# A pre-norm decoder layer on one core: residual rows loaded behind the second weights, cross results stored and norms read back later, weight making begun later, more ternary comparisons in the first batch

## The chip, the cores and the metric

The kernel runs on 1 core of a Trainium2 chip. The core has a matrix engine (PE, TensorE), a vector engine (DVE, VectorE), a scalar engine (ACT, ScalarE), a general engine (POOL, GpSimd) and a synchronising engine (SP, SyncE). Each takes its instructions in the order in which the program gives them to it; a wait holds everything behind it on the same engine. SP and POOL here issue the DMA transfers, which 16 DMA engines carry out. The metric is device time of one execution in microseconds (us), lower is better.

## What is computed

The reference is a decoder layer with a norm ahead of each of its three parts, for x and a context ctx of 4 batches x 512 rows x 512 features, all in 32-bit floats (cut to what matters):

```
x = x + self_attention(layernorm(x))       # 16 heads of 128, Wq Wk Wv Wo with biases
x = x + gamma * cross(layernorm(x), ctx)   # keys and values are both ctx
x = x + ffn(layernorm(x))                  # ternary weights

# self_attention: q, k, v = x @ W + b, shaped (heads, 128, T); the attention runs over
#   the features: att = softmax(q @ k / sqrt(128)) is 128x128 per head; y = att @ v; y @ Wo + bo
# cross: 8 heads over blocks of 64 rows: softmax((q.T @ k) / sqrt(64)), 512x512 per head, times v
# ffn: silu(x @ w1q.T) * (x @ w3q.T), then @ w2q.T, hidden size 1365
# ternary: q = clip(round(w / s), -1, 1) * s with s = mean(abs(w)), for w1, w3 and w2
```

## The kernel before

The work is done in this order, with times of the profile of before.

*First phase, 0 to about 289 us.* Norms of x, Gram matrices, keys and scores of the four batches. Beside it, on "ticks" (a generator is advanced by so many steps at so many places of the main work; the class `Side` counts them), `kept_weights` (L296 to L337) makes the weights Wo and Wv ready: each row piece is loaded by SP (L205), split into a high part h (ACT, L277), a low part l and a third part d (DVE), and the three parts are stored by SP to scratch (`kept`). It is advanced KEPT_STEPS = 64 steps over 80 ticks. `scale_steps` sums the absolute values of the ternary matrices (ACT, L636). PE turns and multiplies the Gram matrices; `gt` (L475) needs the copy of G by ACT (L438).

*The batch loop, about 289 to 820 us* (b = 0 to 3, in each four groups of heads j = 0 to 3). For every (b, j), `values_out` makes the products `pu` with the parts oh, ol, od of Wo, `values_of` makes `pm` with vh, vl, vd of Wv, and `output` (L567 to L573) adds `po` to the four accumulators `acc`. The twelve loads of 256 KB for each product are issued on SP by `weights`, into a pool of 20 buffers. The accumulators start as the rows of x (`accumulators`: four loads on SP) with the bias bo, broadcast by a fifth load of 256 KB and added by DVE (`biased`, L1034). eT, the turned scores, comes back by SP (`turned_kept`). u, ul, ud and m are made by DVE, uh by ACT.

A product has 6 ticks, so a batch has 48. On these ticks three things run beside the main work: the making of ternary weights, the norms of the batch before, and its cross-attention.

- `ternary_steps` (L653 to L670): a load on POOL (L605), two comparisons on DVE (L660, L661), then a step further a store on POOL (L669). In all 70 steps over the 180 ticks from the first product on.
- `row_norms` (L686 to L702): statistics of the accumulators on DVE, a store of the norms on POOL (`norm_a`), and two reads back on POOL (`norms`).
- `cross(b)` (L704 to L845): all its transfers go through POOL (L713): `fetch` loads xd (rows of x) and kd (rows of the context) for a head, `split` makes qs, kh and kl of them with the norms (ACT L733 and L737, DVE L734 and L738), `softmax_rows` does the scores `xs` (PE L750, L751), their maximum (DVE), the exponentials p (ACT L761) and the division, `transpose_rows` turns p (PE, then a copy to pt by ACT L131 or DVE L133), `turn_values` turns the rows `keys` into `vals` (one buffer), `weigh_values` multiplies them (`xo`, L794) and adds the residual rows `xc` (DVE L802), and `store` writes the result to x_c. Every 4 scores make one such result; c counts the results, `phase` the scores in it. The loads `keys` and `xc` share one kind of buffer ("late").

The last cross-attention and the feed-forward part (L1183, L1192, L1221) run from about 820 to 1141 us.

The parts of the order around the change that matter: SP issues in the order acc, bo, weights vh.. of the first product, eT, weights oh.. of the second one; POOL issues in the order in which the generators are advanced.

Of the kernel before, what the change touches and what calls it, by code (L numbers as in the profile page):

```python
# [19 lines left out]
P = 128  # L20
B, T, D = 4, 512, 512
NC = T // P
KC = D // P
# [18 lines left out]
def decoder_layer_kernel(  # L42
# [161 lines left out]
    def load(dst, src):  # L204
        nc.sync.dma_start(dst, src)  # L205
        return dst
# [89 lines left out]
    def kept_weights(pool):  # L296

        def items():
            for j in range(HG):
                for k in range(KC):  # L300
                    yield "o", j, k, None
                for k in CHUNKS:
                    yield "v", j, k, None

        sources = {}

        def bring(n, j, k):
            if n == "o":
                t = pool.tile([P, GW], F32, tag="raw_v", bufs=4, name=f"o_raw_{j}_{k}")
                load(t, by_group(wo[j * T : (j + 1) * T, :], k))  # L310
                return t
            if k == KC - 1:
                sources[j] = raw_of("v", j, pool, load, 4)
            return sources[j][1](k)

        coming = []
        for item in itertools.chain(items(), [None, None]):
            if item is not None:
                coming.append((item[:3], bring(*item[:3])))
                if len(coming) < 3:  # L320
                    continue
            (n, j, k), t = coming.pop(0)
            gate = gates[0]
            if n == "v":
                fold(k, t, sources[j][0], gate)
            tri = Tri(
                *(pool.tile([P, GW], F32R, tag="made", bufs=4, name=f"{n}{p}_{j}_{k}") for p in "hl"),
                t.bitcast(F32R),
            )
            halves_of_weight(tri.h, tri.l, t, gate)  # L330
            third_of_weight(tri)
            yield
            for p, part in zip("hld", (tri.h, tri.l, tri.d)):
                load(kept[n, j, p][ts(k, P), :], part.bitcast(F32))
            yield

    KEPT_STEPS = 2 * 2 * HG * KC  # L337

    def weights(n, b, j, wp):

        def part(p, k):
            t = wp.tile([P, GW], F32R, tag="w", name=f"{n}{p}_{b}_{j}_{k}")
            load(t.bitcast(F32), kept[n, j, p][ts(k, P), :])
            return t

        halves = [(part("h", k), part("l", k)) for k in range(KC)]
        return [Tri(*halves[k], part("d", k)) for k in range(KC)]
# [327 lines left out]
    def each(steps, stp):  # L675
        for name in MATRICES:
            yield from steps(stp, name)
# [8 lines left out]
    def row_norms(b, accs):  # L686


        mv = small.tile([P, NG, 2], F32, tag="mvc", bufs=2, name=f"mv_c_{b}")
        for g in range(NG):  # L690
            yield
            moments(mv[:, g, :], accs[g], f"c_{b}_{g}")
        rstd = rstd_of(mv, f"c_{b}")
        mean, var = (mv[:, :, i : i + 1].rearrange("p c s -> p (c s)") for i in range(2))
        nc.vector.tensor_scalar(mean, mean, -1.0, None, ALU.mult)
        nc.vector.tensor_copy(var, rstd)
        nc.gpsimd.dma_start(norm_a[b].rearrange("(p g) s -> p g s", g=NG), mv)
        norms[b] = small.tile([P, 2 * NC, 2], F32, tag="norms", bufs=2, name=f"norms_{b}")
        for half in (slice(0, XD), slice(XD, P)):
            nc.gpsimd.dma_start(norms[b][half], norm_a[b].rearrange("(n p) s -> p n s", p=XD))  # L700
        for _ in range(NG + 3):
            yield  # L702

    def cross(b, cx, cin, cpp, cpt):  # L704
# [11 lines left out]
        def late(name, src):  # L716
            return load(cx.tile([P, T], F32, tag="late", name=f"{name}_{b}"), src)
# [70 lines left out]
        def weigh_values(c, xc):  # L788
            pt = [pts.pop(2 * c + j) for j in range(2)]
            po = bank(f"xo_{b}_{c}")  # L790
            for l in range(NC):
                for j in range(2):
                    half = slice(j * XD, (j + 1) * XD)
                    nc.tensor.matmul(  # L794
                        po[half, :],
                        lhsT=vals[c][:, l, half],
                        rhs=pt[j][:, l, :],
                        start=(l == 0),
                        stop=(l == NC - 1),
                    )  # L800
            y = vals.pop(c).rearrange("p l d -> p (l d)")
            nc.vector.scalar_tensor_tensor(y, po, gam, xc, ALU.mult, ALU.add)  # L802
            return lambda: load(x_c[b][ts(c, P), :], y)
# [14 lines left out]
        for i in range(len(order) + 3):  # L818
            c, phase = divmod(i, 4)
            if phase == 3 and c < NC:  # L820
                rows[c] = late(f"keys_{c}", kv[b][ts(c, P), :])
            if i < len(order):
                ps[order[i]] = softmax_rows(*order[i])
            if i < len(order):
                yield
            if phase == 2 and c > 0:
                store = weigh_values(c - 1, rows.pop(c - 1))
                yield
            if 2 <= i < len(order) + 2:
                n, h = order[i - 2]  # L830
                transpose_rows(n, h, ps.pop((n, h)))
            if i % 2 == 0 and i // 2 + 1 < heads:
                split(i // 2 + 1)
            if i % 2 == 0 and i // 2 + 2 < heads:
                fetch(i // 2 + 2)
            if phase == 2 and c > 0:
                store()
            if i < len(order) + 2:
                yield
            if phase == 0 and c > 0:  # L840
                turn_values(c - 1)
            if phase == 1 and c > 0:
                rows[c - 1] = late(f"xc_{c - 1}", x_a[b][ts(c - 1, P), :])
            if i < len(order) + 2:
                yield  # L845
# [177 lines left out]
    def accumulators(b):  # L1023
        accs = []
        for g in range(NG):
            acc = accp.tile([P, D], F32, tag="acc", name=f"acc_{b}_{g}")
            load(acc, by_group(x[b], g))
            accs.append(acc)
        return accs
# [5 lines left out]

    PRODUCT = 6
    TICKS = 2 * HG * PRODUCT
    quant, aside, side = Side(), Side(), Side()
    waiting, accs = None, None

# [11 lines left out]
    def turning():  # L1052
        count = itertools.count(1)

        def tick():
            at = next(count)
            if at in (4, 6):
                turn(len(STEPS) - 4 + at // 2)

        return tick  # L1060

    for b in range(B):
        for j in range(HG):
            if b == 0 and j == 0:
                wo_tiles = weights("o", b, j, wp)
                accs = accumulators(0)
                load(bo_bc, bo.to_broadcast([P, D]))
            else:
                if j == HG - 1 and b + 1 < B:
                    next_accs = accumulators(b + 1)  # L1070
                wo_tiles = weights("o", b, j, wp)
            u3 = values_out(b, j, x3, wo_tiles, tick if b + j > 0 else turning())
            if b == 0 and j == 0:
                quant = Side(each(ternary_steps, stp), 2 * PIECES, B * TICKS - 2 * PRODUCT)
            if waiting:
                output(*waiting)
            if j == 0 and b > 0:
                aside.rest()
                crossing = itertools.chain(row_norms(b - 1, accs), cross(b - 1, *cpool))
                aside = Side(itertools.islice(crossing, AHEAD), AHEAD, (3 if b == 1 else 2) * PRODUCT)  # L1080
                accs = next_accs
            if j == 1 and b > 1:
                begin_cross(TICKS)
            if j == HG - 2:
                xs = rows_kept(b + 1, xnp, "xn")
            if j == HG - 1 and b + 1 < B:
                x3 = parts_of(b + 1, xs)
            elif j == HG - 1:
                for t in xs:
                    settle(t)  # L1090
                ffn_0 = prepare_ffn(0, xs)
                for _ in range(NC):
                    next(ffn_0)
            wv_tiles = weights("v", b, j, wp)
            eT = turned_kept(b, j)
            ms = values_of(b, j, wv_tiles, u3, tick)
            if j == 0:
                biased(accs)
            if j == 1 and b == 1:
                begin_cross(TICKS - PRODUCT)  # L1100
            waiting = [b, j, eT, ms, accs]
# [177 lines left out]
```

## Time and profile before

| | us |
|---|---|
| three runs | 1147.08, 1142.03, 1145.89 |
| median of them | 1145.89 |
| profiled execution, its own time | 1143.08 |
| its span in the profile | 1141.3 |
| PE busy | 1124.5 |
| DVE, ACT, POOL busy | 808.1, 562.4, 204.1 |

The profiled execution lies 2.81 us below the median of the runs, and its span 1.8 us below its own time. An engine's busy time leaves out waits; the weight loads of PE (PEld) run beside its products. In a list of waits a row names the engine and line that waited, what ended the wait last, and then total us, number and longest. A timeline row gives start, duration, engine, line, operation, output and inputs, the number of instructions joined in the row, and in brackets the idle time before the first of them with what ended it. SPq and the rows of POOL with DMA_DIRECT2D are issues of transfers; a transfer lands some us later.

The 16 DMA engines are 90% and more busy in many of the 40 slices of the first 830 us, 70 to 80% in most others (q1, the queue of SP, carries 187.48 MB, q0, that of POOL, 63.50 MB over the whole span), and mostly 10 to 20% busy after that.

### The profile page before, as it was taken

What the parts mean: (1) busy time and instruction counts of PE and PEld (TensorE: products, weight loads), DVE (VectorE), ACT (ScalarE), POOL (GpSimd) and SP (SyncE); (2) the same over time, 40 slices, a digit from 0 to 9 for tenths busy, and PEclk for the clock granted to TensorE, in tenths of its full rate; (3) what the DMA queues carried; (4) which work ended last, traced back from release to release, by engine and by line L of the source; (5) the groups of instructions that cost most, each with busy time, mean ns of one, the idle gap of its engine ahead of it and who ended that gap; (6) DMA issues with size and microseconds to landing.
All of it is one profiled execution on the core that took longest, in us unless ns stands there. A gap on an engine that the chain in (4) does not pass through costs nothing.

```text
span 1141.3 us, 16617 instructions
## 1 busy us (share of the span) xinstructions
PE 1124.5 (99%) x5406; PEld 874.1 (77%) x5406; DVE 808.1 (71%) x1616; ACT 562.4 (49%) x1200; POOL 204.1 (18%) x377
## 2 busy tenths in 40 slices
PE   9999999999999999999999999999999999999998
PEld 6778888888777777777767777577677877778886
DVE  7678676865556786898778788696887669537252
ACT  5375545553322334665646565465566557434020
POOL 2011001010111132232223213221222212000000
PEclk9999999999999999999999999999999999999999
DMA  9257879794999899978779977896941422121200
GB/s 308 80 177 242 277 251 327 241 326 149 386 351 384 302 316 332 332 231 299 240 221 333 319 235 255 252 332 224 328 152 65 148 65 65 47 74 37 93 1 37
DMA packets 145844, 252.04 MB, mean 221 GB/s; under 512 B 17032, under 2 KB 48008, under 8 KB 145758
## 3 DMA queue, kind: packets, MB, share of 16 engines
q1 hardware_dynamic: 124830, 187.48, 48.6%
q0 software_dynamic: 20928, 63.50, 17.4%
q8 instruction: 43, 0.70, 0.2%
q14 instruction: 43, 0.35, 0.1%
HBM read 196.37 MB, written 54.54 MB: 220 GB/s over the span
## 4 chain that ended last, share of the span: by engine, by line
PE 80%; DMA 7%; DVE 5%; issue 5%; ACT 2%; POOL 1%; SPq 0%; POOLq 0%; DVEq 0%; ACTq 0%
PE h L1183 13%; PE y L1221 7%; PE sc L529 5%; PE xo L794 4%; PE xp L128 4%; PE po L570 3%; PE xs L750 2%; PE xs L751 2%; DMA kd<-in_kv_dram 2%; PE pm_2d L368 1%; PE pu_0h L357 1%; PE pm_3h L356 1%; PE pu_3h L356 1%; PE pu_0d L368 1%; PE py_3h L356 1%
## 5 line engine op out<-in xcount | busy, mean ns | idle before, releaser
L1183 PE MATMUL h<-fxh,t 128*128 128x512 f32 (+1 forms) x352 | 139.8, 397 | 0.0
L1183 PE MATMUL h<-fxl,t 128*128 128x512 f32 (+1 forms) x352 | 137.5, 390 | 0.0
L761 ACT ACTIVATE p<-xs,xnmax 128x512 f32<-128x512 f32 x128 | 86.9, 686 | 94.9 <-PE xp L128 55.2
L755 DVE TENSOR_REDUCE xnmax<-xs 128x1 f32<-128x512 f32 x128 | 84.7, 681 | 2.8 <-PE xs L751 2.8
L1183 PEld LDWEIGHTS h<-fxh,t 128*128 128x128 f32 (+1 forms) x352 | 65.0, 185 | 16.4 <-issue 1.9
L1183 PEld LDWEIGHTS h<-fxl,t 128*128 128x128 f32 (+1 forms) x352 | 65.0, 185 | 14.6 <-DVE fxl L141 0.4
L1221 PE MATMUL y<-t,gh 128*128 128x512 f32 (+1 forms) x176 | 69.3, 394 | 0.0
L1221 PE MATMUL y<-t,gl 128*128 128x512 f32 (+1 forms) x176 | 68.8, 391 | 0.0
L128 PEld LDWEIGHTS xp<-ident,p 128*128 128x128 f32 x512 | 59.0, 140 | 11.2 <-issue 2.4
L131 ACT COPY pt<-xp 128x512 f32<-128x512 f32 x96 | 54.3, 590 | 26.5 <-PE xp L128 26.5
L128 PE MATMUL xp<-ident,p 128*128 128x128 f32 x512 | 66.4, 273 | 0.1
L713 POOL DMA_DIRECT2D xd<-x_a x64 | 33.7, 531 | 169.5 <-DVE qs L734 112.8
L1192 ACT ACTIVATE th<-h,scales_w 128x512 f32<-128x512 f32 (+1 forms) x44 | 30.4, 691 | 65.7 <-PE h L1183 65.5
L529 PE MATMUL sc<-y,q_raw 128*128 128x128 f32 x512 | 59.3, 275 | 0.0
L529 PEld LDWEIGHTS sc<-y,q_raw 128*128 128x128 f32 x512 | 58.4, 192 | 0.2
L570 PE MATMUL po<-m,eT 128*128 128x512 f32 x128 | 58.1, 595 | 0.4 <-DVE u L378 0.4
L794 PE MATMUL xo<-pt,vals 128*64 128x512 f32 x256 | 58.5, 598 | 0.0
L197 ACT ACTIVATE uh<-u 128x512 fp32r<-128x512 f32 x64 | 40.2, 632 | 28.2 <-DVE u L378 28.1
L750 PE MATMUL xs<-kh,qs 128*128 128x512 f32 x128 | 51.1, 400 | 2.1 <-DVE vals L802 1.4
L669 POOL DMA_DIRECT2D t_w<-tern_w x43 | 28.6, 666 | 125.1 <-DVE tern_w L661 117.7
L751 PE MATMUL xs<-kl,qs 128*128 128x512 f32 x128 | 50.1, 391 | 0.0
L773 ACT ACTIVATE p<-p,xrden 128x512 f32<-128x512 f32 x64 | 47.1, 736 | 4.3 <-DVE xrden L771 3.9
(243 smaller groups left out, 2841.4 us busy)
## 6 DMA issues: line engine op xcount, KB each, us to landing
oh<-kept_oh SPq DMA_DIRECT2D x64, 256.0 KB, 6.6
ol<-kept_ol SPq DMA_DIRECT2D x64, 256.0 KB, 7.2
od<-kept_od SPq DMA_DIRECT2D x64, 256.0 KB, 5.2
vh<-kept_vh SPq DMA_DIRECT2D x64, 256.0 KB, 6.4
vl<-kept_vl SPq DMA_DIRECT2D x64, 256.0 KB, 6.5
vd<-kept_vd SPq DMA_DIRECT2D x64, 256.0 KB, 4.6
xd<-x_a POOLq DMA_DIRECT2D x64, 128.0 KB, 5.5
kd<-in_kv_dram POOLq DMA_DIRECT2D x64, 128.0 KB, 6.1
```

What stands on the lines that cost most here:

```text
L128: nc.tensor.transpose(pt[:, ts(k, P)], src[:, ts(k, P)], ident)
L131: nc.scalar.copy(dst, pv)
L529: nc.tensor.matmul(sc[:, ts(g, DH)], lhsT=w[k][:, ts(g, DH)], rhs=ys[k][:, ts(g, DH)], start=(k == 0), stop=(k == KC - 1),)
L570: nc.tensor.matmul(po, lhsT=eT[:, ts(g, DH)], rhs=ms[g], start=True, stop=True)
L750: nc.tensor.matmul(sc, lhsT=q[:, ts(m, P)], rhs=kh, start=True, stop=False)
L751: nc.tensor.matmul(sc, lhsT=q[:, ts(m, P)], rhs=kl, start=False, stop=True)
L755: nc.vector.reduce_max(nmax[:, i : i + 1], scs[i], axis=AX.X)
L761: nc.scalar.activation(p, scs[i], AF.Exp, bias=nmax[:, i : i + 1], scale=xscale, accum_out=den[:, i : i + 1],)
L773: nc.scalar.mul(ps[1], ps[1], rden[:, 1:2])
L794: nc.tensor.matmul(po[half, :], lhsT=vals[c][:, l, half], rhs=pt[j][:, l, :], start=(l == 0), stop=(l == NC - 1),)
L1183: nc.tensor.matmul(ph[:r, :], lhsT=t[:, block(i, k)], rhs=fxT[j][:, k, :], start=(k == 0 and j == 0), stop=(k == KC - 1 and j == 1),)
L1221: nc.tensor.matmul(py, lhsT=g[i][j][:r, ts(c, P)], rhs=t2[:r, i, :], start=(i == 0 and j == 0), stop=(i == NHC - 1 and j == 1),)
```

## The change

The change moves work to other places of the program, in five parts:

1. In `kept_weights` the first two pieces, which are loaded with nothing made yet, now yield two steps each, so everything that is made comes later in the ticks; KEPT_STEPS grows by 4 to 68, over the same ticks.
2. In the first product of the batch loop, the four loads of the accumulators and the one of bo leave their place ahead of the first weights of Wv and come behind the weights oh, ol, od of the second product (b = 0, j = 1); the bias is then added by DVE there, ahead of the first `output`, instead of after the first product's `values_of`.
3. In `row_norms`, three steps now lie between the store of the norms and their reading back; the steps after it are three fewer.
4. In `cross`, the store of a result comes at the start of the next phase (behind the loading of `keys`), not at the end of the phase that made it; for the last result it is at once.
5. Of the ternary steps, 20 run over the first 36 ticks, then, from the second batch on, 50 over 144 ticks.

```
@@ kept_weights
                 if len(coming) < 3:
+                    yield
+                    yield
                     continue
-    KEPT_STEPS = 2 * 2 * HG * KC
+    KEPT_STEPS = 2 * 2 * HG * KC + 4
@@ row_norms
         nc.gpsimd.dma_start(norm_a[b].rearrange("(p g) s -> p g s", g=NG), mv)
+        for _ in range(3):
+            yield
         norms[b] = small.tile([P, 2 * NC, 2], F32, tag="norms", bufs=2, name=f"norms_{b}")
         for half in (slice(0, XD), slice(XD, P)):
             nc.gpsimd.dma_start(norms[b][half], norm_a[b].rearrange("(n p) s -> p n s", p=XD))
-        for _ in range(NG + 3):
+        for _ in range(NG):
             yield
@@ cross
             if phase == 3 and c < NC:
                 rows[c] = late(f"keys_{c}", kv[b][ts(c, P), :])
+            if phase == 3 and c > 0:
+                store()
...
             if phase == 2 and c > 0:
                 store = weigh_values(c - 1, rows.pop(c - 1))
+                if c == NC:
+                    store()
                 yield
...
-            if phase == 2 and c > 0:
-                store()
@@ the batch loop
+    FIRST_STEPS = 20
...
             if b == 0 and j == 0:
                 wo_tiles = weights("o", b, j, wp)
-                accs = accumulators(0)
-                load(bo_bc, bo.to_broadcast([P, D]))
             else:
                 if j == HG - 1 and b + 1 < B:
                     next_accs = accumulators(b + 1)
                 wo_tiles = weights("o", b, j, wp)
+                if b == 0 and j == 1:
+                    accs = accumulators(0)
+                    load(bo_bc, bo.to_broadcast([P, D]))
+                    waiting[4] = accs
             u3 = values_out(b, j, x3, wo_tiles, tick if b + j > 0 else turning())
             if b == 0 and j == 0:
-                quant = Side(each(ternary_steps, stp), 2 * PIECES, B * TICKS - 2 * PRODUCT)
+                ternary = each(ternary_steps, stp)
+                quant = Side(ternary, FIRST_STEPS, TICKS - 2 * PRODUCT)
+            if b == 1 and j == 0:
+                quant = Side(ternary, 2 * PIECES - FIRST_STEPS, (B - 1) * TICKS)
+            if b == 0 and j == 1:
+                biased(accs)
...
             ms = values_of(b, j, wv_tiles, u3, tick)
-            if j == 0:
+            if j == 0 and b > 0:
                 biased(accs)
```

## The prediction

> **What bounds the kernel now.** I read the page first, then the waits of TensorE (PE), then the timelines around each wait.
>
> ```profile
> span 1141.3 us, 16617 instructions
> ## 1 busy us (share of the span) xinstructions
> PE 1124.5 (99%) x5406; PEld 874.1 (77%) x5406; DVE 808.1 (71%) x1616; ACT 562.4 (49%) x1200; POOL 204.1 (18%) x377
> ```
>
> PE is busy for 1124.5 of 1141.3 us. The change takes no matrix product away, so it can win only out of the 16.8 us in which PE isn't busy, or lose by adding to them. The list of what PE waited for:
>
> ```profile
> PE vt L128 <- DMA keys<-in_kv_dram: 2.9, 2, 1.8
> PE gt L475 <- ACT G L438: 2.0, 1, 2.0
> PE pu_1h L357 <- DMA ol<-kept_ol: 1.5, 1, 1.5
> PE pm_1h L356 <- ACT p L761: 1.5, 1, 1.5
> PE xs L750 <- DVE vals L802: 1.4, 1, 1.4
> ```
>
> Few waits, each 1 to 2 us, each naming a place that the change touches. The waits leave out what a start-up costs, so I price each place by the excess of the distance between two matmul starts over the usual distance of that form: 2.2 us at 76.42, 1.67 at 313.05, four short ones of 0.58, 0.80, 0.52 and 0.50 between 444.8 and 463.28, 1.98 at 565.77, 1.65 at 587.32, 1.19 at 714.87, 1.60 at 732.38. That is 12.7 us, all that I think the change can reach. The granted clock is 1.00 in every stretch, so nothing moves by the clock.
>
> **The change part by part.** It removes and adds no arithmetic and no bytes: as many loads, comparisons and bias additions as before, in other places of each engine's order. So each term is a wait.
>
> *Weight making two steps later* (place 1, 76.42). ACT works in order:
>
> ```profile
> 76.71 0.72 ACT L277 ACTIVATE oh<-o_raw,gate 128x512 fp32r<-128x512 f32 x1 [1.96 <-DMA o_raw<-in_wo_dram]
> ...
> 78.56 0.62 ACT L438 COPY G<-gt 128x128 f32<-128x128 f32 x2
> ```
>
> ACT stood 1.96 us for a row of wo and then did the first oh (0.72), one sum of absolutes (0.61) and the second oh (0.71, at 77.95) before the copy of G that PE waited for. In the new order of ACT one oh and no second one stands before that copy, and the sum stands before the oh, in the time when ACT idled. 78.56 becomes 76.71 + 0.63 = 77.34: 1.2 us. Bounds: 0 (the loads come as late as ACT does) to 2.0 (oh gone from there). I take 1.2. The later rows have until 285 us: no PE wait stands between 80 and 285.
>
> *Residual rows and bo behind the second weights* (place 2, 313.05). SP's queue:
>
> ```profile
> 287.88 2.24 SPq L205 DMA_DIRECT2D acc<-in_x_dram  x4
> 290.54 0.33 SPq L205 DMA_DIRECT2D bo_bc<-in_bo_dram  x1
> ...
> 301.59 0.32 SPq L205 DMA_DIRECT2D eT<-kept_e  x1
> ...
> 307.78 0.32 SPq L205 DMA_DIRECT2D ol<-kept_ol  x1
> ```
> ```profile
> 314.95 0.50 PE L357 MATMUL pu_1h<-ol,xl 128*128 128x512 f32 x1 [1.51 <-DMA ol<-kept_ol]
> ```
>
> The five loads of 256 KB took the queue from 287.88 to the next load at 291.13: 3.25 us, 0.65 each. The last ol of the second weights left at 307.78, after 2.4 us in which SP waited for an older transfer, because everything ahead was late; PE got it 1.51 us late. Without the five ahead the backlog at 300 us is gone. The load of eT itself stays where it is (301.59, its buffer comes free then), but lands sooner, so ol goes out near 305 and lands near 310: the whole 1.67 us goes. Bounds: 0 (the issue is held by eT's buffer as before) to 1.67; I take 1.5. The five now stand ahead of the next vh, issued at 311.18 before: they take 3.25 us there, and SP reaches them 2.7 us sooner (307.78 against 305.1), so vh is some 0.5 us late against a use at 326.56 and a landing 8.2 us after issue (311.18 to 319.41): 7 us of cover. The four bias additions (2.49 us in the row at 560.14) move into DVE's run of 323.57 to 329.88; they take the slots of the four evictions, which follow. The next row of DVE had 2.58 us idle before it (332.46), which covers them by 0.1; gone, it would cost the m rows 0.1 us for each 0.1. Costed at nothing.
>
> *More comparisons in the first batch* (place 3). Twenty steps over 36 ticks instead of fourteen, 24 by the swap. Batch 0 has DVE idle (3.69 at 318.81, 2.97 at 337.90, 4.14 at 343.33) and a pair costs 0.48 + 0.75 us: hidden. In the next batch, the loads of tern_w3_0 to 2 leave POOL (426.11 to 429.6), and DVE no longer idles 3.33 us before the comparison at 433.97, which kept the first qs until 435.28. The xd that waited for it (436.32, 6.71 us) goes out 1.3 us sooner and the next kd 2.3 us. Of the 2.4 us here I take 0.9, for in the new ACT order the table load and two exponentials (1.28 + 2 x 0.69 us) stand ahead of the copies of pu. Bounds: -1.4 to 2.4. The burst of three w2 loads now falls near 584 instead of 618: 3 x 0.65 us less the 0.55 that an issue takes, at worst 1.4; I take -0.3.
>
> *Cross results stored, norms read back later* (places 4 to 7). POOL's queue in the second of these batches:
>
> ```profile
> 552.02 1.40 POOL L700 DMA_DIRECT2D norms<-norm_a  x2 [1.41 <-DMA norm_a<-mv_c]
> 553.41 0.57 POOL L713 DMA_DIRECT2D xc<-x_a  x1
> ...
> 560.38 0.56 POOL L713 DMA_DIRECT2D x_c<-vals  x1 [5.65 <-ACT pt L131]
> 560.93 0.55 POOL L605 DMA_DIRECT2D tern_w<-in_w3t_dram  x1
> 561.48 0.55 POOL L713 DMA_DIRECT2D keys<-in_kv_dram  x1
> ```
>
> xc waits behind the norms' trip (550.07 to 553.41), lands at 559.06, and only then does the addition of L802 run (559.08, DVE idle 1.28); the store behind it holds POOL 5.65 us, and keys, last, land at 567.84, 1.98 us late for PE. In the new order xc stands right behind norm_a (550.61, so 2.8 us sooner), and keys ahead of the store. The addition runs by 557, keys leave by 558.5 and land near 564.9, before PE needs them at 566: 1.9 (bounds 0 to 1.98). At 714.87 keys were behind the norms, the store and a load; without the store they leave at 706.9 against 708.0 and have 256 KB less ahead (0.65): 1.1 of 1.19 (bounds 0 to 1.19). At 587.32 PE waited for the exponentials, these for DVE's qs at 585.40, ACT having stood for xd (3.79) and kd (1.64) and DVE's four accumulations (2.48) being ahead; in the new order qs and kl come ahead of the four and the xd leaves sooner: 1.5 (-0.5 to 1.65). At 732.38 the chain began with POOL held to 710.35 by a comparison at 709.32 to 710.05; in the new order that place has a comparison done before 700, so xd leaves at 708.6, 2.3 us sooner: 1.2 (0 to 1.60).
>
> The norms themselves: they landed at 421.90, 556.65 and 712.44 and DVE first read them at 423.70, 564.77 and 714.29. Their issue is tied to norm_a's landing (416.18, 551.74, 704.95), not to the position, as long as nothing put between waits; the issues put between (1.28, 1.33 and 0.56 us) fit into POOL's waits for that landing (4.71, 1.41, 3.02). The stores of x_c come later by an issue or two; the buffer's next copy came 4.79 us or more after the landing of its store. Costed at nothing.
>
> On these transfers the Trainium skill, "DMA: Bandwidth & Descriptors", section "Issuing engines are not separate DMA queues", speaks against the change: the queues of all engines share the same 16 DMA engines and interleave, so a load moved from one queue's stretch burdens whatever the other sends there. The trace bears it out: a 128 KB kd took 7.16 us from issue to landing (572.49 to 579.65) beside SP's loads, and 2.67 with few of them (588.22). The page's own fit (section "Anatomy of one DMA") would give an estimate of 2.0 + 131072/436000 = 2.3 us; by it place 5 would win the wait whole, and by the row a mere reordering saves only what leaves sooner. The sum goes without it.
>
> **The sum.** 1.2 + 1.5 + 0.9 - 0.3 + 1.9 + 1.1 + 1.5 + 1.2 = 9.0 us. The profiled execution took 1143.08 us, the span and 1.8 around it; 1143.08 - 9.0 = 1134.1. The median shown, 1145.89, is 2.8 above it, so on that scale 1136.9: 1137. The low ends add to -1.4 - 1.4 - 0.5 = -3.3, a loss, the high ends to 12.5, a gain.
>
> **The rivals.** *Only the plain queue positions win.* For it: places 3, 5 and 7 hang on ACT and DVE in order and on transfers of 6 to 8 us, and one freed wait may turn into the next. Then 1.2 + 1.5 + 1.9 = 4.6 less up to 1.4 for the burst: 3.2 to 4.6, time 1141.3 to 1142.7. Against it: the heads of those chains do leave 1.3 to 2.8 us sooner.
>
> *The change doesn't do what it says.* SP never has more than some eight loads out and stops at eT's buffer, POOL stops for data: if the waits are set by these and not by position, the same waits come again: 1144 to 1147. Against it: xc and the five loads stood ahead for 2.8 and 3.25 us, which no buffer asked for.
>
> *Slower: the norms wait behind a comparison.* POOL has six waits of a ternary store for its comparison, up to 8.1 us, 25.7 together. If the store now ahead of the norms' reading waits like that, the norms come 8.1 us late at 423.70, where 1.80 us is the cover: 6.3 us on DVE and so on PE; in the next batch the cover of 8.1 holds for the norms, but keys and xd behind them are late by up to 8.1 less the 2.8 gained: 5.3. With places 1 and 2 won (2.7) it is 8.9 slower: 1154.8. It decides where such a store leaves after 418.3. Against it: in the new DVE order those comparisons stand before the statistics are done (410.75).
>
> **How the numbers follow.** The forecast 0.52, the first rival 0.26, no effect 0.12, slower 0.10. What can be told from no change is 0.5%, 5.7 us: faster is below 1140.2. The forecast gives faster, of the first rival 0.10 too (its top with a quieter run); the same is 0.16 + 0.12 = 0.28; slower 0.10. The range goes from 1145.9 - 12.5 and 2 us for a quick run, 1131, to 1146, which takes in the first rival and no effect; the forecast's own is 1133 to 1140.
>
> **What would show it.** Right: PE's waits for ol, for keys and for G (to under 1 us) gone or small, xc behind norm_a, the L802 of 559 us some 2 us sooner, PE's time outside busy near 8 us. Wrong: DVE idle for norms, a new wait of PE for vh, vals or ul, or as much idle time in other places.

## The result, and the profile after

The changed kernel takes 1156.56 us (median of 6 runs, 1153.83 to 1158.71), the kernel before 1144.82 (6 runs): ratio 1.0103, 95% interval 1.008 to 1.0126. So it is 1.0% slower, clear of noise. I had forecast 1137 and a range up to 1146. The sign was wrong.

The first lines of the page of the changed kernel:

```profile
span 1156.1 us, 16618 instructions
## 1 busy us (share of the span) xinstructions
PE 1132.5 (98%) x5406; PEld 880.7 (76%) x5406; DVE 806.9 (70%) x1616; ACT 562.2 (49%) x1200; POOL 203.9 (18%) x377
```

The span is 14.8 us longer. PE does the same 5406 products, but is busy 8.0 us longer (1132.5 against 1124.5), and not busy for 23.6 us instead of 16.8, 6.8 more. So there are two losses: waits, and slower products. The list of what PE waited for:

```profile
PE xp L128 <- ACT p L765: 2.2, 1, 2.2
PE pu_2h L358 <- ACT p L765: 2.0, 1, 2.0
PE xs L754 <- DVE vals L806: 1.9, 1, 1.9
PE tot_w L646 <- ACT kh L277: 1.8, 1, 1.8
PE xp L128 <- ACT p L777: 1.8, 1, 1.8
PE vt L128 <- ACT p L765: 1.6, 1, 1.6
PE pu_1d L370 <- DMA od<-kept_od: 1.5, 1, 1.5
PE gt L477 <- ACT G L440: 1.2, 1, 1.2
```

Read it against the list of before: the waits for keys are gone, that for ol has shrunk to 0.8 us and one of 1.5 for od has come; waits for ACT's exponentials (p) now lead. The excess between matmul starts was 12.7 us at seven places; now it is 21.7: 1.40 at 77, 1.99 at 138, 1.02 at 165, 1.01 and 1.67 at 316 and 318, 1.03 near 372, 1.21 at 412, 2.51 from 454, 2.39 at 479, 1.77 and 2.32 from 576, 0.57 at 602, 2.78 from 745.

The slower products show in the granted clock. Here are stretches of the changed kernel of 3.41 us each. The columns are: stretch, length, then PE, PEld, DVE, ACT and POOL busy (with the number of instructions), granted clock, share of the DMA engines, GB/s.

```profile
316.30:319.71 3.41, 1.10 (x4) 0.65 (x5) 0.00 (x0) 1.07 (x2) 1.81 (x3) 1.00 1.04 361
452.84:456.25 3.41, 1.42 (x7) 0.86 (x5) 2.12 (x4) 2.47 (x5) 1.60 (x3) 1.00 1.07 340
575.72:579.13 3.41, 1.71 (x9) 0.97 (x7) 1.43 (x3) 2.19 (x6) 0.00 (x0) 1.00 0.77 228
579.13:582.54 3.41, 1.69 (x9) 1.72 (x9) 3.35 (x7) 3.13 (x7) 0.00 (x0) 0.51 0.55 169
746.35:749.77 3.42, 1.56 (x7) 1.18 (x7) 3.41 (x6) 0.04 (x1) 0.89 (x2) 1.00 0.00 0
135.39:138.80 3.41, 2.61 (x12) 1.83 (x10) 2.61 (x7) 1.45 (x2) 0.00 (x0) 1.00 0.98 334
138.80:142.21 3.41, 2.38 (x11) 2.02 (x12) 3.41 (x9) 3.10 (x11) 0.00 (x0) 1.00 0.12 38
476.73:480.14 3.41, 2.27 (x13) 1.67 (x11) 0.94 (x2) 1.07 (x2) 0.00 (x0) 1.00 1.04 295
480.14:483.55 3.41, 2.32 (x12) 1.95 (x13) 1.61 (x4) 3.14 (x8) 0.19 (x1) 1.00 0.78 285
...
456.40:459.80 3.40, 3.40 (x10) 2.55 (x9) 3.25 (x7) 2.32 (x6) 0.00 (x0) 0.51 1.06 280
```

After each of the first five stretches, in which PE was busy for 1.10 to 1.71 us, the clock is 0.50 for the next 3.4 us (the last row shows one of them, 0.51 in 456.40 to 459.80). After the four stretches from 135.39 to 480.14, with 2.27 us or more, it stays at 1.00. The half-clock stretches begin at 319.8, 456.3, 579.2 and 749.8: distances of 136.5 (40 times 3.413), 122.9 (36 times) and 170.6 (50 times). So they lie on a grid that runs on by itself. The wait of 2.39 us at 479 and that of 1.99 at 138 lie across a line of the grid and cost no clock; the 2.16 at 454 lies within one stretch and does. The Trainium skill, "TensorE: Matmul & The Clock Gate", section "What's actually happening", has this window: 3413 ns, running free of the kernel. That agrees with the distances. Its section "Why this matters for your kernels" allows idle gaps of up to some 3 us; here 1.7 to 2.3 us of idleness in one stretch was enough, and the measurement decides.

The profiles of all twenty kernels of this case bear the grid out: fifteen have half clock, 37 stretches of it in all, each exactly one stretch of 3.413 us of its execution's grid. At full clock, every one of the 20 grid stretches in which PE was busy for 1.53 us or less was followed by half clock, and none with 1.88 us or more; of those between, 12 were and 9 were not, so PE's busy time alone does not decide there. Where the grid falls differs from one execution to the next: the same wait for G near 78 us (2.0 to 2.6 us) is followed by half clock in the profiles of e2, e3, e9, e17 and e18 below, and not in those of before, e4, e5, e7, e12, e13, e15 and e16.

A half-clock stretch costs 1.7 us (half of 3.4) where PE is busy. There are five of them (PE was busy for 1.69 us in the one at 579 and throughout the others), an estimate of 4 x 1.7 + 0.8 = 7.6: most of the 8.0 us of longer busy time. Below I take a run apart by its span and its mean granted clock: "clock loss" is span x (1 - clock), "clock-free span" is span x clock. The kernel before, in 35 runs beside the first experiments: mean time 1144.2, clock loss 1.7, clock-free span 1140.7 (standard deviation of one run 1.2). The changed kernel, 6 runs: 1156.5, 6.5, 1148.2. So of 12.3 us, 7.5 are waits and 4.8 clock.

### The profile page after: what moved, and what is told of

Same layout as the page of the kernel before. It is cut to its first block, busy times and chain, and to the rows that moved or that the text cites. A ratio compares the mean times of both kernels' runs of the same rounds, so it can differ in the third digit from the quotient of the medians.

```text
span 1156.1 us, 16618 instructions
## 1 busy us (share of the span) xinstructions
PE 1132.5 (98%) x5406; PEld 880.7 (76%) x5406; DVE 806.9 (70%) x1616; ACT 562.2 (49%) x1200; POOL 203.9 (18%) x377
## 4 chain that ended last, share of the span: by engine, by line
PE 67%; issue 11%; DMA 9%; DVE 7%; ACT 2%; POOL 1%; SPq 1%; POOLq 0%; ACTq 0%; DVEq 0%
PE h L1197 14%; PE y L1235 7%; PE xp L128 4%; PE xo L798 3%; DMA kd<-in_kv_dram 3%; PE po L572 3%; PE sc L531 2%; PE xs L754 2%; PE xs L755 2%; DMA od<-kept_od 1%; PE py_3h L358 1%; PE py_2h L358 1%; PE py_3h L359 1%; PE py_2h L359 1%; PE py_3d L370 1%
## 5 line engine op out<-in xcount | busy, mean ns | idle before, releaser
L777 ACT ACTIVATE p<-p,xrden 128x512 f32<-128x512 f32 x64 | 47.0, 735 | 5.8 <-DVE xrden L775 5.5
```

The source lines that it names most:

```text
L777: nc.scalar.mul(ps[1], ps[1], rden[:, 1:2])
```

## The experiments

All figures are means over the runs of a kernel; the ratio is against the kernel before on the same chip, with its 95% interval.

| | time | clock loss | clock-free span | ratio (95% interval) |
|---|---|---|---|---|
| before (35 runs) | 1144.2 | 1.7 | 1140.7 | |
| changed (6 runs) | 1156.5 | 6.5 | 1148.2 | 1.0103 (1.008 to 1.0126) |
| e1 part 1 alone | 1145.9 | 2.3 | 1141.8 | 1.0013 (0.9998 to 1.0027) |
| e2 part 2 alone | 1143.3 | 1.6 | 1139.8 | 0.999 (0.9977 to 1.0002) |
| e3 part 3 alone | 1144.6 | 2.5 | 1140.3 | 1.0003 (0.9991 to 1.0015) |
| e4 part 4 alone | 1144.8 | 2.7 | 1140.3 | 1.0006 (0.9993 to 1.0018) |
| e5 part 5 alone | 1155.6 | 7.7 | 1146.1 | 1.0106 (1.0088 to 1.0123) |
| e6 without part 5 | 1149.0 | 5.2 | 1142.0 | 1.0046 (1.0029 to 1.0063) |
| e7 without part 1 | 1156.9 | 9.1 | 1146.1 | 1.0117 (1.0093 to 1.014) |
| e8 without part 2 | 1156.3 | 7.9 | 1146.7 | 1.0112 (1.0091 to 1.0133) |
| e9 part 5, seamless loads | 1153.0 | 5.8 | 1145.4 | 1.0073 (1.0059 to 1.0088) |
| e10 changed, split behind exponentials | 1149.4 | 4.1 | 1143.5 | 1.0042 (1.0029 to 1.0056) |
| e11 changed, three waits filled | 1160.9 | 2.6 | 1156.5 | 1.0145 (1.0128 to 1.0162) |
| e12 before, seamless loads | 1142.7 | 1.9 | 1139.1 | 0.9981 (0.9969 to 0.9993) |
| e13 part 5, both remedies | 1143.6 | 2.2 | 1139.7 | 0.9992 (0.9982 to 1.0003) |
| e14 changed, both remedies | 1144.2 | 1.7 | 1140.8 | 1.0 (0.9988 to 1.0013) |
| e15 before, split behind exponentials | 1140.1 | 0.8 | 1137.5 | 0.9958 (0.9944 to 0.9973) |
| e16 before, both remedies | 1140.3 | 2.4 | 1136.1 | 0.9962 (0.9948 to 0.9975) |
| e17 part 2, both remedies | 1139.1 | 1.5 | 1135.8 | 0.995 (0.9932 to 0.9969) |
| e18 parts 2 to 4, both remedies | 1139.0 | 1.9 | 1135.3 | 0.9956 (0.994 to 0.9971) |

The runs of e1 to e18 were taken on five chips, and the kernel before differs between them: its mean is 1144.2 us beside e1 to e4, 1143.5 beside e5 to e8, 1144.9 beside e9 to e12, 1144.1 beside e13 to e16 and 1143.9 beside e17 and e18. So times of different groups are best compared by their ratios, or each as its difference from its own before.

### Each part alone

*e1*, the later weight making:

```
                 if len(coming) < 3:
+                    yield
+                    yield
                     continue
...
-    KEPT_STEPS = 2 * 2 * HG * KC
+    KEPT_STEPS = 2 * 2 * HG * KC + 4
```

> Only the later weight making (part 1) is done. Theory (the loss is made of new PE waits that each part makes for itself, plus half clock behind some of them): the wait for G at 76 us shrinks from 2.2 to 1.4 us and a new wait of 2.0 for the sums of w1 at 138 and of 1.0 for y at 165 come, as in the changed kernel: 2.2 us slower than before, no half clock. Rival (the loss is made only where parts meet, the order of the engines being planned anew): within 1 us of before. My prediction on record: 1.2 us faster.

Measured: the wait for G fell from 2.22 to 0.83 us, more than I had forecast, and a wait of 2.30 came at 137, with a half-clock stretch behind it in the profiled execution; that at 165 did not come. 1.7 us slower in the mean, just short of what the interval tells from nothing. The new wait is the sum of absolutes of w1: its reduction on DVE stands behind the making of an oh, and ACT stood 7.85 us for the store of an older vh before that one (at 135.32). The piece I had costed at nothing, "the later rows have until 285 us", ignored that DVE and ACT do other work behind them.

*e2*, the residual rows and bo:

```
             if b == 0 and j == 0:
                 wo_tiles = weights("o", b, j, wp)
-                accs = accumulators(0)
-                load(bo_bc, bo.to_broadcast([P, D]))
...
+                if b == 0 and j == 1:
+                    accs = accumulators(0)
+                    load(bo_bc, bo.to_broadcast([P, D]))
+                    waiting[4] = accs
```

> Only the residual rows and bo behind the second weights (part 2). Theory: eT is still loaded only when its buffer comes free (302 us), so ol is late as before or by 0.7 us less, and od is late by 1.7 us because the five loads share the DMA engines with it; these two waits together bring 3.4 us of half clock: 1 us of waits and 1.7 us of clock, 2.7 us slower than before. Rival (the od wait comes from the ternary part's loads): the ol wait goes and it is 1.5 us faster, as predicted on record.

Measured: ol was late by 0.69 us. No product waited for od, but the weight loads of od's products did (PEld, 1.1 us, against 0.5 before), and eight of these products took 2.47 us from start to start instead of 1.82: od was late by some 0.65 us. The time is 0.9 us less, not clear of noise. So this part alone makes little of the od wait (e8 says the same), and my 1.5 us were 1.0.

*e3* (norms read back three steps later) and *e4* (the store later):

```
+        for _ in range(3):
+            yield
         norms[b] = small.tile([P, 2 * NC, 2], F32, tag="norms", bufs=2, name=f"norms_{b}")
...
-        for _ in range(NG + 3):
+        for _ in range(NG):
```
```
+            if phase == 3 and c > 0:
+                store()
...
-            if phase == 2 and c > 0:
-                store()
```

> Only the norms read back three steps later (part 3). Theory: the split of the first head comes in another place of ACT's order, kh ahead of the exponentials, and PE waits for these at the second and third such batch: two waits of 1.6 to 2 us more, and half clock behind them (3.4 us), 3 to 5 us slower than before. Rival (the store part does that): xc leaves sooner and the wait for keys at 566 us goes, 2 us faster.

> Only the cross results stored later (part 4). Theory: keys leave ahead of the store, so the waits for keys at 566 and 715 us shrink by 1 to 2 us each: 1.5 to 3 us faster than before. Rival: the exponentials are behind kh or qs in ACT's order and it is slower by 3 us.

Measured: in both the waits for keys at 566 and 715 go, as forecast, and others take their place: in e3 1.19 us at 568 and 1.56 at 582, and 2.79 instead of 1.60 at 732; in e4 1.71 at 567 and 2.04 at 732. Both are at the time of before. Neither expectation held in its size.

*e5*, the pace:

```
+                ternary = each(ternary_steps, stp)
+                quant = Side(ternary, FIRST_STEPS, TICKS - 2 * PRODUCT)
+            if b == 1 and j == 0:
+                quant = Side(ternary, 2 * PIECES - FIRST_STEPS, (B - 1) * TICKS)
```

> Only the ternary pace (part 5): 20 steps over the first 36 ticks. Theory A (this part makes the loss alone): waits of 1.2 us for ul at 411, 2 us for the copy behind the exponentials at 453 and 2.4 us at 479, and half clock behind them; with the loads' burst moved, 8 to 12 us slower than before, since the four other parts alone gave -1 to +2. Theory B (the parts make the loss only together, for each new place in an order meets the waits that the other part left): within 2.5 us of before.

Measured: 1155.6, the time of the whole change, 12.1 us above the kernel before on the same chip. Theory A held: the part whose place I had put down as a gain of 0.6 us (+0.9 and -0.3) makes the loss alone. Its DVE rows near 400 and 595 us:

```profile
392.70 1.29 DVE L378 SCALAR_TENSOR_TENSOR m<-pm_3t,pm_3d 128x512 f32<-128x512 f32 x2 [0.92 <-PE pm_3d L368]
400.47 0.49 DVE L660 TENSOR_SCALAR above_w<-tern_w,scales_w 128x512 bf16<-128x512 f32 x1 [6.47 <-DMA tern_w<-in_w3t_dram]
...
594.99 0.49 DVE L660 TENSOR_SCALAR above_w<-tern_w,scales_w 128x512 bf16<-128x512 f32 x1 [3.27 <-DMA tern_w<-in_w2t_dram]
```

DVE stands 6.47 and 3.27 us. These are the first pieces of w3 and w2: where a new matrix begins, three loads are issued in a burst, and the first comparison is the next step, right behind its own load. Behind it, in DVE's order, is what PE waits for next. For the second one PE's row says it:

```profile
598.54 0.50 PE L356 MATMUL pm_1h<-uh,vh 128*128 128x512 f32 x1 [3.46 <-ACT p L761]
```

The comparison ended at 596.2, the maxima, the exponentials and the product followed. Before the change, such a stand (3.33 us at 433.97) was there too, in a place where it cost PE little. In the whole change the two stands are 6.39 us (at 402.42) and 3.15 (at 599.36), and PE waits only 1.04 us (at 413.18) and 0.41 (at 602.91) behind them.

### Parts taken out

*e6* to *e8* are the changed kernel without parts 5, 1 and 2 (the diffs above, left out).

> The change without part 5. Theory A: as the sum of the four parts alone, 1 to 3 us slower than before. Theory B: 5 us or more slower than before, with the waits at 576 and 579 us there and those at 411, 453 and 479 too or in other places.

> The change without part 1. Both theories: the waits at 138 (2.0 us) and 165 (1.0) go and the wait for G is 2.2 again: clock-free span 1.5 to 2.5 us below the changed kernel's 1148.2. Rival (the ol and od waits at 316 depend on the making as well): 4 us or more below.

> The change without part 2. If the five loads, now beside od, made the od waits at 318 and 371 us: these go and the ol wait of 1.7 us stays: 1 to 3 us below the changed kernel and one half-clock stretch (1.7 us) fewer. Rival (od is late for other reasons, the earlier comparisons' loads): no faster than the changed kernel.

Measured: without the pace 1149.0, above 1147, and 5.4 above its own before (1143.5), more than the sum of four parts (their mean times differ from 1144.2 by +1.7, -0.9, +0.4 and +0.6, 1.8 together). It has the two waits from 570 on (2.07 and 1.97) and 3.0 us at 738, more than parts 3 and 4 alone: those two do meet. So B holds too: the four lose some 3.6 us more together than one by one. The pace alone (12.1) and the other four together (5.4) make more than the whole change loses (11.8 by the two medians), so their costs overlap. Without part 1 the clock-free span fell by 2.1 as expected, but the clock loss rose by 2.6: no gain in time. Without part 2 the od wait at 318 was 1.99: the five loads don't make it, the pace does (e5 alone: 1.95 at 315), and the rival was right.

### What costs the time

The order in which ACT has its work is planned from all parts together. Before, ACT did the copies of pu ahead of the first exponentials at 447; with the pace moved, behind them. With the pace alone (e5), ACT's rows and PE's near 475 us are these:

```profile
473.44 0.72 ACT L733 ACTIVATE qs<-xd,norms 128x512 fp32r<-128x512 f32 x1 [2.33 <-DMA xd<-x_a]
476.35 0.72 ACT L737 ACTIVATE kh<-kd,norms 128x512 fp32r<-128x512 f32 x1 [2.19 <-DMA kd<-in_kv_dram]
476.98 0.67 ACT L761 ACTIVATE p<-xs,xnmax 128x512 f32<-128x512 f32 x1
...
477.79 0.66 PE L128 MATMUL xp<-ident,p 128*128 128x128 f32 x4 [2.32 <-ACT p L761]
```

The split of a head (qs, kh) waits twice for its loads, the exponentials stand behind it, and PE waits 2.32 us for them. In the kernel before the split stood ahead of those exponentials too, but ACT stood only 1.28 us for kd there (at 468.73), and PE has no wait listed: here the loads come later, and the order is the same. In the whole change the order is another one as well. Around 572 us of it (ACT's rows; the last is of the kernel before):

```profile
571.84 1.07 ACT L365 COPY pu_1t<-pu_1h 128x512 f32<-128x512 f32 x2 [0.74 <-PE pu_1h L359]
576.95 0.72 ACT L741 ACTIVATE kh<-kd,norms 128x512 fp32r<-128x512 f32 x1 [4.03 <-DMA t_w<-tern_w]
577.57 0.67 ACT L765 ACTIVATE p<-xs,xnmax 128x512 f32<-128x512 f32 x1
...
565.06 0.69 ACT L761 ACTIVATE p<-xs,xnmax 128x512 f32<-128x512 f32 x1 [2.76 <-DVE norms L617]
```

kh needs kd, which left at 568.4 to 569.7; ACT stands 4.03 us for it, and the exponentials behind it, whose maxima were done at 573.25, come 4 us late (the releaser that the row names landed then; kd's landing is the wait). Before the change, at 565.06, the same exponentials stood ahead of the split of that head. This place is of the other four parts together and not of the pace: e6, without the pace, has the same order (kh at 570.36, 4.33 us for kd), and e5, e3 and e4 have not. So the mechanism is one, and both the pace and the other parts set it off. Two remedies, one for DVE's stands and one for ACT's:

*e9*, the loads run on over the seam of two matrices, and *e10*, a head's split held behind the exponentials:

```
-        s = scales[name]
-        for piece, t, i in ahead(stp, pieces_of(name), f"tern_{name}", 2):
+        pieces = [(src, (name, t)) for name in MATRICES for src, t in pieces_of(name)]
+        for piece, (name, t), i in ahead(stp, pieces, "tern", 2):
+            s = scales[name]
```
```
-                nc.scalar.activation(
+                mark["exp"] = nc.scalar.activation(
                     p,
...
-                )
+                ).ins
...
-            with tc.issue_after(mark["copied"]):
+            with tc.issue_after(mark["copied"]), tc.issue_after(mark.get("exp", mark["copied"])):
                 nc.scalar.activation(q, xd, AF.Identity, bias=less)
```

> Part 5 alone, but the loads run two pieces ahead over the seam of two matrices, so a matrix no longer begins with three loads in a burst and a comparison right behind them. Theory (the moved pace costs because DVE, in order, stands 6.5 us at 400 us and 3.3 at 595 for the first load of w3 and of w2, at places where u and the row maximum are behind it): these two waits of DVE go, and with them PE's 1.3 us at 410 and 3.6 at 595: the clock-free span 4 to 5 us below the 1146.1 of part 5 alone, the time 5 to 8 us below its 1155.6. Rival (the earlier comparisons' work or the loads' traffic makes the loss): within 2 us of part 5 alone.

> The changed kernel, with the split of a head (qs, kh on ACT) held behind the exponentials traced before it. Theory (ACT, in order, stands for kd or xd with exponentials behind it that PE waits for): the waits at 479 (2.4 us) and 579 (2.0) go, that at 453 (2.2) shrinks: clock-free span 4 to 6 us below 1148.2, and fewer half-clock stretches (6.5 us lost before, 3 to 4 here): 6 to 9 us faster than the changed kernel's 1156.5. Rival (the exponentials are late by themselves): no faster.

Measured: e9 took the two stands of DVE away (the one at the start, 2.8 us for w1, is left), PE's wait at 410 went and that at 595 fell from 3.62 to 1.53; but the clock-free span fell by 0.7 only and the time by 2.6 against e5 (1.3 and 4.0 when each is set against its own before), between theory and rival: waits for exponentials at 451 (1.90) and 474 (2.54) were as before. e10 took away exactly those: no wait at 454, 479, 577 to 579 and only 0.57 of 2.78 near 745. 7.1 us faster than the changed kernel (1156.5), as expected. Left was the comparison of w2, now 4.22 us at 590.

*e11* put work into the waits:

```
+        if name in ("vt_0_3", "xp_0_7_1_0"):
+            for _ in range(16):
+                nc.tensor.matmul(pt[:, :P], lhsT=ones, rhs=ones, start=True, stop=True)
...
+            if name == "pu_0_1" and pair == (0, 1):
+                for _ in range(16):
+                    nc.tensor.matmul(pd[0][:, :P], lhsT=ones, rhs=ones, start=True, stop=True)
```

> The changed kernel, with 16 products of ones (1.8 us of PE) put right ahead of three instructions that PE waits for 1.7 to 2 us: the first pu with od at 318, the turn of keys at 576, the turn of p at 579. They are overwritten. Theory (half clock follows a stretch of some 3.4 us in which PE was idle for most): the waits stay, PE is busy in them, and three of the four or five half-clock stretches go, 1.7 us each: clock loss from 6.5 us to 1.5 to 3, time 3 to 5 us below the changed kernel's 1156.5. Rival (half clock has another cause, as the load of the chip): no change of the loss, and the time the same or up to 3 us longer.

Measured: the clock loss fell from 6.5 to 2.6, to none in the profiled execution: half clock does follow PE's idleness. The time was missed, for two reasons that the row of PE shows:

```profile
578.33 3.84 PE L129 MATMUL vt<-ones 128*128 128x128 f32 x32 [1.45 <-ACT p L771]
```

The 16 products run as 32 instructions, 3.84 us and not 1.8; and they waited themselves, for the exponentials that free their buffer. Filling is no remedy here.

*e13* and *e14* have both remedies, in part 5 alone and in the whole change (both diffs above together).

> Part 5 alone with both remedies: loads run on over the seam, and the split behind the exponentials. Theory (the pace costs because it moves comparisons and so shifts ACT's order, which then puts a wait for kd ahead of exponentials, and because two comparisons wait for their own load): both gone, the clock-free span falls from 1146.1 to 1141 to 1143 and the clock loss from 7.7 to 2 to 4: 1143 to 1147. Rival (the traffic of the earlier loads delays SP's od and ol at 315 and is the larger part): 1149 or more.

> The whole change with both remedies. Theory: as the split behind the exponentials (1149.4 mean), less the wait of 4.2 us at 590 for the comparison of w2 and that of 1.4 at 410: clock-free span 1139 to 1141, time 1143 to 1146. Rival (a planned order that is held at one place breaks at another): 1148 or more.

Measured: 1143.6 and 1144.2, the time of before. PE's longest waits in e14:

```profile
PE tot_w L646 <- ACT kh L277: 1.7, 1, 1.7
PE pu_1h L359 <- DMA ol<-kept_ol: 1.7, 1, 1.7
PE xo L799 <- ACT pt L131: 1.1, 1, 1.1
```

No exponentials are among them. But the kernel before gains by the same remedies (next), so the right comparison is e13 with e16: 1143.6 against 1140.3. Of the 12.1 us that the pace costs (1155.6 against 1143.5 before, on one chip), 8.8 go by ACT's order, the two comparisons, and the clock behind them; 3.3 stay. What these are is open. In the profile of e13 SP's weights are late: od by 1.46 us at 316 (0.62 in e16), 0.53 and 0.50 near 367 (none in e16). But this doesn't last: PE of e13 is 2.5 us behind that of e16 at 374 us, 0.1 at 609 and some 0.7 at 820. Most of the difference of these two executions comes between 841 and 852 us, in the last cross-attention. PE's rows of the same products in e13 and, last, in e16:

```profile
851.54 3.65 PE L795 MATMUL xo<-pt,vals 128*64 128x512 f32 x14 [1.14 <-ACT pt L131]
...
847.62 3.65 PE L795 MATMUL xo<-pt,vals 128*64 128x512 f32 x16
```

In e13 POOL stood 2.86 us there before it issued a kd (at 846.57), with nothing in the profile that it waited for; e14 has the same stand (at 846.54) and the same wait of PE (1.12 us). Why, no run shows. Nor does a run test by itself whether the earlier comparisons' loads are what delays od.

### A faster kernel

*e12*, *e15* and *e16* are the kernel before with the seamless loads, with the split behind the exponentials, and with both; *e17* adds part 2, *e18* parts 2 to 4 (diffs above).

> The kernel before with the loads run on over the seam of two matrices. The DVE wait of 3.3 us at 434 goes, and the one for w2; the waits of PE between 445 and 463 (2.4 us in all) may go with it: 0 to 2.5 us faster than before. Rival: the waits there are made by kd, which lands at 446: within 0.5 us.

> The kernel before with the split held behind the exponentials. In it ACT stood 3.8 and 1.6 us for xd and kd at 577 to 580 and 4.0 and 2.1 at 727 to 730, with exponentials behind them. Theory: PE's waits at 587 (1.65) and 732 (1.6) go, 2 to 4 us faster than before. Rival (the exponentials there need the same kd): within 1 us of before.

> The kernel before with both remedies: seamless loads gave 1.5 us; with the split behind the exponentials 3 to 6 us faster than before. Rival: no faster than the seamless loads alone (1142.7).

> The kernel before with part 2 (the residual rows and bo behind the second weights) and both remedies. Part 2 alone took 0.9 us off. If the parts add up: 1139 to 1140 mean, 4 to 5 us faster than before. Rival: the ol wait at 315 comes back in another form and it is no faster than both remedies alone (1140.3).

> Parts 2, 3 and 4 of the change (without the later making and without the pace) and both remedies. If the later reads of the norms and the later stores, my places 4 to 7, are worth what I forecast once ACT's order is held: 1136 or less. If they are worth nothing, as alone: 1139 to 1141. Rival (they move the order again): above 1142.

Measured: holding ACT's order alone takes 4.1 us off the kernel before, clear of noise, and its clock loss falls to 0.8. PE's waits of e15 between 550 and 740 us:

```profile
PE vt L128 <- DMA keys<-in_kv_dram: 2.5, 2, 1.8
PE pu_2h L356 <- ACT pu_2t L363: 0.7, 1, 0.7
```

The waits at 587 and 732 are gone; those for keys, which the order has nothing to do with, stay. The seamless loads take 2.1 off alone (1142.7 against 1144.9 on the same chip), and add nothing to the other (e16). Parts 2 to 4 on top give another 1.0 us (e18 is 4.9 under its own before, e16 3.9), part 2 alone as much (e17, 4.8): no interval separates them. So with ACT's order held, parts 3 and 4 add nothing to part 2 that can be seen; places 4 to 7 of the prediction, a forecast of 5.7 us, are not in the time, as the expectation's "1139 to 1141" said for that case. e17 and e18 are the fastest seen, 0.4 to 0.5% under the kernel before. The sum closes: e18 (1139.0), part 1 alone (1.7) and the 3.3 us of the pace that stay make an estimate of 1144.0, and e14 took 1144.2, though on another chip than e18 and e1.

## Why the prediction was wrong

Point by point, by its own steps:

- *Place 1*: the wait shrank, 2.22 to 1.40 (forecast 1.2, came 0.8). The step "the later rows have until 285 us" failed: waits of 1.99 and 1.02 us came at 138 and 165.
- *Place 2*: the five loads went, and ol stayed late by 1.01 us. I had seen that eT's load holds the queue and took the better bound. SP's rows of the changed kernel:

```profile
296.24 2.33 SPq L205 DMA_DIRECT2D vd<-kept_vd  x4
304.24 0.32 SPq L205 DMA_DIRECT2D eT<-kept_e  x1
304.66 0.40 SPq L205 DMA_DIRECT2D oh<-kept_oh  x1
```

 SP was free from 298.6 and stood until 304.24: the time won by the moved loads was spent waiting for eT's buffer. PE itself was 3.0 us later by then (pm_0h starts at 301.98, before at 298.94), so eT came free at the same point of the work as before. That was my second rival, at this one place.
- *Place 3, the step that failed*: "a pair costs 0.48 + 0.75 us: hidden". In the sum the place was a gain of 0.6 us (+0.9 and -0.3); part 5 alone lost 12.1 us (e5). I priced the comparisons' work and not what they wait for. What the runs showed in its place: comparisons that hold DVE until their own loads land (6.47 and 3.27 us), exponentials on ACT behind a split that waits for its loads (PE 2.32 us at 477.79), and a clock loss of 7.7 us where before has 1.7; with both remedies 8.8 of the 12.1 us are gone. The burst at the seam I did see, and priced it as traffic (-0.3); the comparison right behind it holds DVE for 6.4 us in the changed kernel too. And I read in the new order that the table load and two exponentials stood ahead of the copies of pu, and took it as less gain (0.9 of 2.4) where it is a wait of 2.16 us of its own, with half clock behind it.
- *Place 4*: xc did leave right behind norm_a (561.49 after 560.96) and the wait was not for keys any more; but in its place vt now waited 1.77 for the exponentials behind kh, and xp 1.97 for the division that follows them (L777). *Place 7*: 2.78 instead of 1.60, the same kind by way of DVE: PE's xs waits 1.86 us for DVE's addition (L806), which stands behind kl, and kl waits for ACT's kh, before which ACT stood 3.10 us for xd and 2.82 for kd; with ACT's order held 0.57 is left (e10). I had looked at where each transfer leaves, not at what stands behind its first reader on ACT.
- *Places 5 and 6* were right: 1.65 to 0.57 (forecast 0.15), 1.19 to none.
- *The norms*, costed at nothing, were: in the batch loop DVE waited 0.46 us for them (at 432), behind it 1.86 (at 858), where it was 2.39 before. So my slower rival came near in size (1154.8) and was wrong in its mechanism. The first rival's point, that one freed wait may turn into the next, was right; I gave it a price of nothing lost.
- *"Nothing moves by the clock"* was read from one execution of before at 1.00 throughout. 25 of 35 runs of that same kernel had a mean clock under 1.000, and 4.8 of the 12.3 us are clock.

## What to carry to other kernels

Where engines work in order and the order is planned, a moved piece of side work is priced by what it waits for and by who stands behind it on its engine, at its new place, and not by its duration. Read the new order for the first reader of each late transfer: if it stands ahead of work that the busiest engine waits for, hold it back by hand. On a busy PE a wait of some 2 us may cost 1.7 us more in half clock, so several short waits are worth removing, and one execution's clock says little about the next one's.

## What the runs showed of the hardware that was not expected

The spread of the kernel before is in part clock: over 35 runs the standard deviation of a run falls from 1.6 to 1.2 us when its clock loss is taken off, and the ten at a mean clock of 1.000 took 1143.0 us in the mean, the ten at 0.998 1144.5, the two at 0.996 1146.1 and the one at 0.995 1148.1. The clock falls to half for 3.4 us after a stretch of a grid of 3.413 us in which PE was busy for 1.53 us or less (20 of 20 in the twenty profiles), and doesn't after 1.88 us or more; between the two it did after 12 stretches of 21, and what decides there no run shows. And 16 products of 128x128 in 32-bit floats ran as 32 instructions of 0.275 us, 0.12 apart.
